# A cross-attention block on one core of Trainium2: all steps of the kernel in another written order

## The chip, the core and the metric

The kernel runs on one core of a Trainium2 chip. A core has five engines that run side by side and wait for each other by semaphores: TensorE (PE, matrix products into PSUM), VectorE (DVE), ScalarE (ACT), GpSimd (POOL) and SyncE (SP, which here only issues DMA transfers). Each engine works through its own list of instructions strictly in the order in which the program emitted them. The time is the device time of one execution, in microseconds (us); several executions give a median and a spread. A profile is the record of one execution.

## The reference

One layer of cross-attention with a feed-forward part, all in fp32: batch B = 4, length L = 512 of both sequences, width D = 512, 16 heads of 32, inner width 2048.

```python
x = layer_norm(hidden_states, ln1_w, ln1_b)
q = (x @ q_w + q_b).reshape(B, LQ, H, HD).transpose(0, 2, 1, 3)
k = (encoder_hidden_states @ k_w + k_b).reshape(B, LK, H, HD).transpose(0, 2, 1, 3)
v = (encoder_hidden_states @ v_w + v_b).reshape(B, LK, H, HD).transpose(0, 2, 1, 3)
scores = jnp.einsum('bhqd,bhkd->bhqk', q, k) * scale
scores = jnp.where(mask, scores, mask_value)
attn = jax.nn.softmax(scores, axis=-1)
out = jnp.einsum('bhqk,bhkd->bhqd', attn, v)
out = out.transpose(0, 2, 1, 3).reshape(B, LQ, D)
out = out @ cproj_w + cproj_b
hidden = out + residual
y = layer_norm(hidden, ln2_w, ln2_b)
y = jax.nn.gelu(y @ fc_w + fc_b, approximate=True)
y = y @ proj_w + proj_b
return residual + y
```

## The kernel before

**Tiles and stages.** The heads of one batch are done in four groups of four, so there are 16 units (batch × group), numbered 0 to 15; each unit has four blocks of 128 query rows. For each unit the kernel projects keys, values and queries, then for each of the four blocks:

- PE computes the scores of four heads into the four PSUM banks `sc` (L581),
- DVE adds the mask and finds the row minimum in one instruction for each head (L589; the scores are negated, so that minimum is the softmax's maximum), which also frees the bank,
- ACT takes the exponential (L592) and sums it,
- DVE turns the result in squares of 32 × 32, two heads at a time (L600, L607; for every second block also L610, the reciprocal of the sums),
- the turned squares change partitions through 12 DMA transfers on SP (`swap<-swap`, issued by the helper at L329) while POOL copies those that stay (L617),
- and after two blocks PE multiplies with the values (L639), and DVE scales the result (L645).

After the four units of a batch come the output projection (L445) with the residual, the second layer norm, the fully connected layer with gelu (L694, L746), whose result goes to DRAM and is read back (`gd`, L748), and at the end of the program the second projection.

**Products in seven instead of eight.** Most large products (keys and values from the second pair of units on, L524, and the fully connected layer, L694) use one level of the Strassen–Winograd scheme: sums of quarters of the weights (POOL) and of the inputs (POOL or DVE), seven smaller products, which are grouped into a chain in one bank and two more in another bank, and a join, in which ACT copies the growing chain out of PSUM three or four times (L720 or, with a bias, L722) and DVE adds the rest (L332). Each product of the chain after the first waits until ACT has copied what stood there. The last projection uses two levels.

**Layer norms.** The statistics of a row block are two DVE instructions (L343, L344). POOL computes the scale from them (L351, L359; named `ve` and `rs`), DVE normalizes the block (L364), and PE turns it (L371) into PSUM, from which DVE or ACT brings it back with weight and bias (L379, L381). For batches 1 to 3 the first layer norm takes another path: the input is also loaded turned (`x_t`), and its statistics are turned on PE (L394) and sent through DRAM (`sd`, L402) so that SP can load them as rows, with which POOL scales the turned input (L412 and L335).

**What sets the order.** All parts are Python generators that emit one piece of their instructions at each step. One string, `ORDER`, names the pieces: each word is a generator (name and indices), and each time a word stands there, that generator makes its next step.

```python
begun = {}
for token in ORDER.split():
    if token not in begun:
        name, *rest = token.split(":")
        begun[token] = takes[name](*map(int, rest))
    if begun[token] is not None:
        next(begun[token], None)
```

So the string sets at once the order on each of the five engines and on the queues of DMA transfers that SP and POOL issue. Words used below: `u:6:0` scores of unit 6, block 0; `x` minima and exponentials; `r` the 32 × 32 turns; `e` exchanges; `d` POOL's copies; `a` attention product; `k:4`, `v:3` key and value products of a pair of units, `kj`, `vj` their joins; `s1`/`s2`, `r1`/`r2`, `n2`, `t2` statistics, scale, normalizing and turning in the two layer norms; `ts` the turned statistics; `es` the sums over the encoder rows; `f`, `j`, `g` fully connected product, join and gelu.

**Buffers.** PSUM has eight banks: four for scores and a ring of four for everything else, which are taken and freed in the written order. The fully connected results go through a few stage buffers (`st`), which are free again once their transfer to `gd` has landed.

Of the kernel before, what the change touches and what calls it, by code (L numbers as in the profile page):

```python
# [20 lines left out]
P = 128  # L21
# [46 lines left out]
u:1:0 kj:1 vj:1 kj:1 k:1 r:0:3 r:0:3 vj:1 v:1 vj:1 lx:1 wq:3 q:3 s1:1 r:0:3 x:1:0 x:1:0 q:3 x:1:0 x:1:0
u:1:1 e:0:0 e:0:0 le:1 e:0:0 lx:1 s1:1 s1:1 r:1:0 wk:4 lh:0 x:1:1 x:1:1 x:1:1 kj:1 x:1:1 kj:1 r:1:1 r:1:0 d:0:1 q:2
  d:0:1 le:1 es:1 vb:0 le:1 lf:0:3 wk:5 le:1 r1:1 es:1 es:1 es:1  # L70
u:1:2 ts:1 ts:1 e:0:1 e:0:1 x:1:2 r:1:1 r:1:1 x:1:2 r:1:1 e:0:1 ks:2 ts:1 ks:2 ks:2 k:2 a:0:0 q:2 x:1:2 x:1:2 a:0:0
  d:1:0
u:1:3 kj:2 x:1:3 x:1:3 k:2 k:2 kj:2 vj:1 r:1:2 x:1:3 x:1:3 r:1:3 r:1:2
u:2:0 x:2:0 r:1:3 wv:4 lt:1 lt:1 lt:1 e:1:0 lb:1 lb:1 a:0:1 k:2 kj:2 v:2 x:2:0 a:0:1 d:1:0 ks:2 na:1 x:2:0 x:2:0
u:2:1 r:1:3 x:2:1 kj:2 e:1:0 e:1:0 na:1 k:2 a:1:0 wa:1 x:2:1 r:1:3 r:2:0 kj:2 x:2:1 x:2:1 wa:1 na:1 r:2:0
u:2:2 x:2:2 wa:1 wq:4 lt:1 na:1 r:2:1 r:2:1 a:1:0 wa:1 x:2:2 x:2:2 d:1:1 q:4 x:2:2 r:2:1 r:2:1 kj:2
u:2:3 x:2:3 vj:2 x:2:3 wq:5 e:1:1 e:1:1 e:1:1 wk:7 wk:6 wv:5 d:1:1 d:2:0 r:2:2 x:2:3 x:2:3 vs:2 ks:3 vs:2 vs:2 ks:3
  vb:1 e:2:0 e:2:0 q:5 e:2:0 wq:7 d:2:0 vs:2 r:2:3 q:4 r:2:3 r:2:2 a:1:1
u:3:0 x:3:0 v:2 v:2 vj:2 a:1:1 x:3:0 r:2:3 x:3:0 x:3:0
u:3:1 x:3:1 x:3:1 r:2:3 r:3:0 a:2:0 v:2 vj:2 x:3:1 x:3:1 a:2:0  # L80
u:3:2 k:3 r:3:0 r:3:1 x:3:2 x:3:2 vj:2 v:2 q:5 r:3:1 x:3:2 kj:3 x:3:2
u:3:3 r:3:1 vj:2 r:3:1 vj:2 x:3:3 d:2:1 vb:1 ks:3 d:2:1 lf:0:0 wq:6 e:2:1 lh:0 e:2:1 e:2:1 e:3:0 e:3:0 e:3:0 wv:6
  x:3:3 d:3:0 d:3:0 s1:2 r:3:2 x:3:3 x:3:3 r:3:2 q:6 a:2:1
u:4:0 m:1 r:3:3 a:2:1 r:3:3 r:3:3 q:7 k:3 x:4:0 x:4:0 q:6 r:3:3 x:4:0 x:4:0
u:4:1 lx:2 r:4:0 wv:7 lt:2 vs:3 ks:3 a:3:0 k:3 x:4:1 q:7 x:4:1 x:4:1 x:4:1
u:4:2 r:4:0 r:4:1 a:3:0 x:4:2 c:0:1 kj:3 k:3 x:4:2 x:4:2 r:4:1 x:4:2 kj:3
u:4:3 lt:2 d:3:1 d:3:1 cb:0 cb:0 r:4:1 vs:3 vs:3 vs:3 r:4:1 d:4:0 vb:2 s1:2 x:4:3 d:4:0 c:0:1 c:0:0 e:3:1 e:3:1 e:3:1
  r:4:2 x:4:3 kj:3 v:3 k:3 lx:2 lf:0:1 lf:0:0 lf:0:3 lh:0 lh:0 cb:0 cb:0 e:4:0 e:4:0 lx:2 e:4:0 lf:0:2 fs:0:0 c:0:0
  r:4:3 kj:3 s2:0 x:4:3 x:4:3 s1:2 a:3:1 vj:3 v:3 v:3 a:3:1 kj:3 r:4:2 r:4:3 vj:3
u:5:0 v:3 r:4:3 s2:0 s1:2 c:0:2 x:5:0 x:5:0 vj:3 r:4:3 vb:2 fs:0:0 r1:2 x:5:0 wv:8 x:5:0 vj:3 r:5:0  # L90
u:5:1 v:3 x:5:1 vj:3 x:5:1 r:5:0 c:0:2 x:5:1 x:5:1 r:5:1 c:0:3 c:0:3 d:4:1 d:4:1 wk:8 le:2 le:2 wk:9 e:4:1 le:2 le:2
  c:0:0 c:0:1 es:2
u:5:2 a:4:0 ts:2 ts:2 k:4 kj:4 r:5:1 x:5:2 s2:0 x:5:2 x:5:2 s2:0 x:5:2 r:5:1 r:5:1 a:4:0 ks:4 es:2 ks:4 es:2 ks:4 ks:4
  es:2 c:0:3 k:4 r2:0 c:0:2 e:4:1 k:4
u:5:3 kj:4 k:4 kj:4 e:4:1 r:5:2 e:5:0 e:5:0 e:5:0 r:5:2 x:5:3 x:5:3 kj:4 vj:3 x:5:3 a:4:1 x:5:3
u:6:0 n2:0 x:6:0 n2:0 k:4 kj:4 n2:0 n2:0 t2:0:3 t2:0:0 t2:0:3 t2:0:0 t2:0:1 t2:0:2 r:5:3 x:6:0 x:6:0 x:6:0 r:5:3
u:6:1 t2:0:1 a:4:1 r:5:3 t2:0:2 kj:4 y:0 y:0 d:5:0 fs:0:0 fs:0:0 fs:0:1 d:5:0 ts:2 fs:0:1 fs:0:1 fs:0:1 a:5:0 y:0
  f:0:1 f:0:0 r:5:3 y:0 j:0:0 j:0:1 x:6:1 a:5:0 x:6:1 r:6:0 f:0:0 f:0:0 f:0:1 x:6:1 x:6:1 f:0:1 j:0:0
u:6:2 f:0:0 j:0:1 j:0:0 lh:1 lt:2 lt:2 wv:9 lb:2 wq:8 lb:2 e:5:1 e:5:1 d:5:1 d:5:1 na:2 r:6:1 r:6:1 r:6:0 f:0:1 j:0:1
  x:6:2 na:2 e:5:1 lx:3 lf:0:2 wk:10 wq:9 j:0:0 f:0:0 na:2 na:2 j:0:0 x:6:2 j:0:1 r:6:1 wa:2 f:0:2 f:0:1 wa:2 j:0:1  # L100
  x:6:2 r:6:2 x:6:2 g:0:0 wa:2 a:5:1
u:6:3 r:6:1 j:0:0 g:0:0 wa:2 q:9 r:6:2 x:6:3 a:5:1 x:6:3 j:0:1 x:6:3 x:6:3
# [918 lines left out]
```

## Time and profile before

| what | us |
|---|---|
| median of 3 runs | 764.81 |
| the runs | 764.81, 766.98, 762.33 |
| the profiled execution | 765.29 |
| its span (first to last instruction) | 763.5 |
| PE busy | 750.3 |
| DVE busy | 614.5 |
| POOL busy | 431.5 |
| ACT busy | 411.4 |

A span is what the profile covers; the time of an execution is 1.8 us longer here. Rows of a profile name the line, the engine, the operation and the tiles, written `out<-in` and without buffer numbers. Where a row ends in brackets, it gives the idle time of that engine just before, and what ended it. The helpers that add, subtract and load have one line each (L332, L335, L329), so such rows are told apart by their tiles: `pbt` holds keys and queries, `ptt` weights and scores, `xn` row blocks, `swap` the turned exponentials, `ext` the turned inputs, `mix` among others the values and the mask. PE's rows count both passes of an fp32 product.

### The profile page before, as it was taken

How to read it: one execution, taken by the hardware profiler on the slowest of the kernel's cores; microseconds unless marked ns; L12 is line 12 of the kernel's file. 1: busy time of each engine (PE TensorE's matmuls, PEld its weight loads, DVE VectorE, ACT ScalarE, POOL GpSimd, SP SyncE). 2: the span in 40 equal slices, each digit the busy share in tenths (PEclk: the TensorE clock that was granted, in tenths of full speed). 3: DMA queues.
4: the chain of work that ended last, by engine and by line, in shares of the span. 5: the costliest groups of instructions: out<-in, count | busy, mean ns of one | idle time of the engine just before them, and what ended most of it. 6: DMA issues, size and time to landing. Idle time of an engine off the chain costs nothing.

```text
span 763.5 us, 14364 instructions
## 1 busy us (share of the span) xinstructions
PE 750.3 (98%) x4953; PEld 548.2 (72%) x4953; DVE 614.5 (80%) x1238; ACT 411.4 (54%) x981; POOL 431.5 (57%) x473
## 2 busy tenths in 40 slices
PE   9999999989999999999999999999999999999998
PEld 6565444646576656776565776767889999999997
DVE  3799999999889889987969787736688789888773
ACT  2567666455998776868867788732234321111111
POOL 1678866876978496889576566894201122131331
PEclk9999999999999999999999999999999999999999
DMA  6788979886777978695785778799535666688565
GB/s 227 236 242 225 236 201 252 232 230 184 242 200 194 281 204 247 196 281 154 214 245 171 218 256 261 215 254 353 167 131 165 214 209 123 213 184 257 140 123 121
DMA packets 72134, 162.19 MB, mean 212 GB/s; under 512 B 11960, under 2 KB 24656, under 8 KB 70400
## 3 DMA queue, kind: packets, MB, share of 16 engines
q1 hardware_dynamic: 56864, 131.44, 58.5%
q0 software_dynamic: 15056, 29.84, 16.0%
q8 instruction: 39, 0.64, 0.3%
q14 instruction: 31, 0.25, 0.1%
q10 hardware_dynamic: 144, 0.02, 0.0%
HBM read 73.95 MB, written 25.18 MB: 130 GB/s over the span
## 4 chain that ended last, share of the span: by engine, by line
PE 87%; DMA 4%; DVE 3%; ACT 3%; SPq 1%; issue 1%; POOL 0%; DVEq 0%; POOLq 0%; ACTq 0%
PE acc L694 36%; PE sc L694 12%; PE acc L524 9%; PE sc L581 8%; PE acc L445 7%; PE acc L639 6%; PE acc L573 5%; DMA ext<-encT_dram 2%; SPq L329 1%; ACT ptt L592 1%; PE acc L371 1%; DVE ptt L589 1%; PE acc L481 1%; PE acc L492 1%; DMA gd<-st 1%
## 5 line engine op out<-in xcount | busy, mean ns | idle before, releaser
L592 ACT ACTIVATE ptt<-ptt,mn 128x512 f32<-128x512 f32 x256 | 182.9, 716 | 52.8 <-DVE mn L589 52.2
L589 DVE CUSTOM_DVE_ANT_0 ptt<-sc,mix 128x512 f32<-128x512 f32 x256 | 165.4, 678 | 21.3 <-PE sc L581 18.6
L617 POOL COPY swap<-swap 32x1088 f32<-32x1088 f32 x128 | 140.2, 1095 | 36.1 <-DVE swap L610 29.6
L720 ACT COPY st<-acc 128x256 f32<-128x256 f32 x128 | 46.1, 367 | 96.3 <-PE acc L694 85.7
L720 ACT COPY xn<-acc 128x128 f32<-128x128 f32 x100 | 24.1, 267 | 133.0 <-PE acc L694 129.3
L600 DVE STREAM_TRANSPOSE swap<-ptt 128x1024 f32<-128x1024 f32 x64 | 79.0, 1235 | 5.2 <-ACT st L746 1.2
L581 PE MATMUL sc<-pbt 32*128 32x512 f32 x512 | 82.0, 647 | 0.0
L607 DVE STREAM_TRANSPOSE swap<-ptt 128x1024 f32<-128x1024 f32 x64 | 78.3, 1223 | 0.6 <-ACT ptt L592 0.6
L748 POOL DMA_DIRECT2D gd<-st x32 | 23.7, 743 | 86.5 <-ACT st L746 65.7
L694 PE MATMUL acc<-ys,ws 128*128 128x256 f32 x256 | 63.4, 383 | 0.5 <-ACT st L720 0.5
L639 PE MATMUL acc<-swap,mix 128*32 128x256 f32 x1024 | 61.9, 382 | 0.9 <-DMA ext<-x_t_dram 0.6
L573 PE MATMUL acc<-ext,ptt 128*128 128x512 f32 x128 | 58.8, 600 | 1.4 <-DVE mn L589 0.8
L445 PE MATMUL acc<-mix 128*128 128x512 f32 x128 | 58.3, 601 | 0.0
L694 PE MATMUL acc<-yT,pbt 128*128 128x256 f32 x240 | 58.1, 383 | 0.0
L694 PEld LDWEIGHTS acc<-ys,ws 128*128 128x128 f32 x256 | 47.4, 190 | 13.1 <-ACT st L720 4.7
L639 PEld LDWEIGHTS acc<-swap,mix 128*32 128x32 f32 x1024 | 30.4, 109 | 33.5 <-issue 9.7
L694 PEld LDWEIGHTS acc<-yT,pbt 128*128 128x128 f32 x240 | 44.5, 190 | 13.7 <-issue 5.1
L906 POOL DMA_DIRECT2D swap<-xn x18 | 22.4, 1434 | 52.8 <-DVE xn L332 18.7
L592 ACT ACTIVATION_READ_ACCUMULATOR ptt<-ptt,mn 128x1 f32 x256 | 48.3, 189 | 0.0
L906 POOL DMA_DIRECT2D yT<-xn x15 | 18.3, 1547 | 48.5 <-DVE yT L332 17.9
L573 PEld LDWEIGHTS acc<-ext,ptt 128*128 128x128 f32 x128 | 23.3, 190 | 30.9 <-issue 23.3
L445 PEld LDWEIGHTS acc<-mix 128*128 128x128 f32 x128 | 23.2, 190 | 31.0 <-issue 28.6
(163 smaller groups left out, 1601.9 us busy)
## 6 DMA issues: line engine op xcount, KB each, us to landing
swap<-swap SPq DMA_DIRECT2D x384, 136.0 KB, 3.3
gd<-st POOLq DMA_DIRECT2D x32, 512.0 KB, 3.9
swap<-gd SPq DMA_DIRECT2D x12, 1024.0 KB, 6.9
pbt<-fc_w_dram SPq DMA_DIRECT2D x40, 256.0 KB, 4.6
xn<-x_dram SPq DMA_DIRECT2D x32, 256.0 KB, 3.9
ext<-fc_w_dram SPq DMA_DIRECT2D x24, 256.0 KB, 3.7
swap<-xn POOLq DMA_DIRECT2D x18, 256.0 KB, 4.7
ptt<-k_w_dram SPq DMA_DIRECT2D x16, 256.0 KB, 5.2
```

Of the source, the lines that this page charges most:

```text
L445: nc.tensor.matmul(acc, oT[:, g, ts(t, P)], wc[:, g, :], start=(g == 0), stop=(g == NG - 1))
L524: nc.tensor.matmul(out_, i, j, start=(k + t == 0 and not more), stop=(k == 1), skip_group_check=more or t > 0)
L573: nc.tensor.matmul(acc, S["wq", w][:, d, :], xT[:, d, :], start=(d == 0), stop=(d == ND - 1))
L581: nc.tensor.matmul(sc[h], S["qT", w][r, ts(qt, P)], S["kT", w][r, :], start=True, stop=True)
L589: nc.vector.tensor_tensor_reduce(out=s, in0=sc[h], in1=mb, scale=1.0, scalar=FMAX, op0=ALU.add, op1=ALU.min, accum_out=mn)
L592: nc.scalar.activation(s, s, AF.Exp, bias=mn, scale=-1.0, accum_out=S["sums", w][:, qt, h : h + 1])
L600: nc.vector.transpose(*two_heads[0])
L607: nc.vector.transpose(*two_heads[1])
L617: nc.gpsimd.tensor_copy(pT[ts(i, HD), i], tb[ts(i, HD), i])
L639: nc.tensor.matmul(av[ts(h, HD), : 2 * P].rearrange(shape, **kw), v[:, t, ts(h, HD)], p[t][h], start=(t == 0), stop=(t == NT - 1),)
L694: nc.tensor.matmul(o, x[:, k], w, start=(k == 0 and not more), stop=(k == n - 1), skip_group_check=more)
L720: nc.scalar.copy(g[:, i], S["qa", *key])
```

## The change

The change replaces the string `ORDER`. The words in it are the same, each as often as before; nearly every line of the string has them in another sequence. The new string is three lines longer, so that every line number further down is higher by three (L589 becomes L592, L364 becomes L367, L332 becomes L335, and L592, the exponential, becomes L595). Two lines of it, as they were and as they are:

```diff
 ORDER = """
...
-u:0:0 x:0:0 x:0:0 x:0:0 x:0:0 wk:3 wv:1 lx:2 wq:1 lx:1 pv:1 wv:2 wq:2 lf:0:1 lx:1 wv:3 lc r:0:0 r:0:0
...
-u:6:0 n2:0 x:6:0 n2:0 k:4 kj:4 n2:0 n2:0 t2:0:3 t2:0:0 t2:0:3 t2:0:0 t2:0:1 t2:0:2 r:5:3 x:6:0 x:6:0 x:6:0 r:5:3
...
+u:0:0 pv:1 lc wv:3 lx:1 wq:2 lf:0:1 lx:1 s1:1 x:0:0 x:0:0 x:0:0 s1:1 x:0:0 r:0:0 r:0:0 ks:1 ks:1 ks:1 vb:0 ks:1 es:0
+  es:0 es:0 es:0 m:0 vs:1 vs:1 pv:1 vs:1 vs:1 vb:0 k:1
...
+u:6:0 a:4:1 r:5:3 t2:0:1 kj:4 r:5:2 x:6:0 a:4:1 x:6:0 f:0:1 t2:0:2 f:0:0 j:0:1 x:6:0 x:6:0 j:0:0 t2:0:2 r:5:3
...
```

Three places are shown as the engines get them.

**DVE, the start of the softmax work.** These are the rows around the first minima (`sc` are score banks, `mn` the minimum, `xn` with `st` and `mv` a row block with its statistics). Before:

```order
L379 TENSOR_SCALAR ext<-acc_78,vec 128x512
L459 TENSOR_SCALAR mix<-m_73 128x512
L567 TENSOR_SCALAR qb<-vec 128x4
L379 TENSOR_SCALAR ext<-acc_78,vec 128x512
L589 ISA ptt,mn_0_0_223<-sc_74,mix 128x512
L589 ISA mn_0_0_223 128x1
L589 ISA ptt,mn_0_1_226<-sc_75,mix 128x512
L589 ISA mn_0_1_226 128x1
L589 ISA ptt,mn_0_2_229<-sc_76,mix 128x512
L589 ISA mn_0_2_229 128x1
```

Now:

```order
L382 TENSOR_SCALAR ext<-acc_81,vec 128x512
L462 TENSOR_SCALAR mix<-m_73 128x512
L570 TENSOR_SCALAR qb<-vec 128x4
L346 BN_STATS st_1_0_254<-xn_86 128x6
L347 BN_AGGR mv_1_253<-st_1_0_254 128x2
L592 ISA ptt,mn_0_0_258<-sc_74,mix 128x512
L592 ISA mn_0_0_258 128x1
L592 ISA ptt,mn_0_1_261<-sc_75,mix 128x512
L592 ISA mn_0_1_261 128x1
L592 ISA ptt,mn_0_2_264<-sc_76,mix 128x512
L592 ISA mn_0_2_264 128x1
L346 BN_STATS st_1_1_267<-xn_87 128x6
```

The statistics of two row blocks of the second batch have moved here, one ahead of the first minimum and one between the third and the fourth (the row that begins it stands last); before, the first of them came behind the twelfth minimum.

**SP, the loads of the second half of the first batch.** The exchanges of the turned exponentials (`swap<-swap`) stand among weight loads, the turned input (`x_t`) and the statistics rows (`sd`). Before:

```order
L329 DMA swap<-swap 32x1088 x12
L329 DMA ptt<-v_w_dram 128x512
L329 DMA ext<-x_t_dram 128x512 x3
L329 DMA swap<-swap 32x1088 x4
L329 DMA xn_87<-sd_99 128x512
L329 DMA xn_82<-sd_99 128x512
L329 DMA swap<-swap 32x1088 x8
L329 DMA ptt<-q_w_dram 128x512
L329 DMA ext<-x_t_dram 128x512
```

Now:

```order
L332 DMA swap<-swap 32x1088 x12
L332 DMA ext<-x_t_dram 128x512
L332 DMA pbt<-fc_w_dram 128x512
L332 DMA ext<-x_t_dram 128x512
L332 DMA xn_86<-sd_99 128x512
L332 DMA xn_87<-sd_99 128x512
L332 DMA swap<-swap 32x1088 x12
L332 DMA ext<-x_t_dram 128x512 x2
L332 DMA ptt<-q_w_dram 128x512 x2
L332 DMA swap<-swap 32x1088 x12
```

The two loads of `sd` stood between four and eight exchanges of one set and now stand ahead of all twelve of it, with loads of `x_t` on both sides. On POOL, the store of `sd` (L402) was issued behind the last three of the four sums over the encoder rows and a weight sum; it now stands behind the first of those four.

**DVE and PE at the second layer norm of the first batch.** On DVE these are minima, the joins of the fifth key pair (L332 with `pbt`) and the normalizations (L364 with `rs`, the scale). Before:

```order
L589 ISA ptt,mn_3_0_1441<-sc_74,mix 128x512
L589 ISA mn_3_0_1441 128x1
L589 ISA ptt,mn_3_1_1444<-sc_75,mix 128x512
L589 ISA mn_3_1_1444 128x1
L332 TENSOR_TENSOR pbt<-acc_78,pbt 128x2x256
L332 TENSOR_TENSOR mix<-acc_79,mix 128x256
L589 ISA ptt,mn_3_2_1449<-sc_76,mix 128x512
L589 ISA mn_3_2_1449 128x1
L589 ISA ptt,mn_3_3_1468<-sc_77,mix 128x512
L589 ISA mn_3_3_1468 128x1
L364 TENSOR_SCALAR xn_85<-xn_85,mv_0_1200,rs_0_1406 128x512
```

Now:

```order
L592 ISA ptt,mn_3_0_1430<-sc_74,mix 128x512
L592 ISA mn_3_0_1430 128x1
L592 ISA ptt,mn_3_1_1433<-sc_75,mix 128x512
L592 ISA mn_3_1_1433 128x1
L367 TENSOR_SCALAR xn_82<-xn_82,mv_0_1257,rs_0_1424 128x512
L367 TENSOR_SCALAR xn_84<-xn_84,mv_0_1257,rs_0_1424 128x512
L367 TENSOR_SCALAR xn_87<-xn_87,mv_0_1257,rs_0_1424 128x512
L335 TENSOR_TENSOR pbt<-acc_78,pbt 128x2x256
L367 TENSOR_SCALAR xn_85<-xn_85,mv_0_1257,rs_0_1424 128x512
L592 ISA ptt,mn_3_2_1481<-sc_76,mix 128x512
L592 ISA mn_3_2_1481 128x1
```

The first three normalizations moved from behind the join to ahead of it, directly behind two minima. On PE, at the same place, are the products of the fifth key pair (L524 with 256 columns), scores (L581) and the turns of the normalized rows (L371). Before:

```order
L524 MATMUL acc_80<-mix,ws_110 128x256 x2
L639 MATMUL acc_81<-swap,mix 32x256 x16
L581 MATMUL sc_74<-pbt 128x512
L581 MATMUL sc_75<-pbt 128x512
L581 MATMUL sc_76<-pbt 128x512
L581 MATMUL sc_77<-pbt 128x512
L524 MATMUL acc_80<-ext,ws_110 128x256 x2
L524 MATMUL acc_78<-mix,ptt 128x256 x2
L371 MATMUL acc_79<-ident,xn_85 128x128
L371 MATMUL acc_79<-ident,xn_83 128x128
L371 MATMUL acc_79<-ident,xn_82 128x128
```

Now:

```order
L397 MATMUL acc_79<-ident,sx_1352 8x128
L527 MATMUL acc_78<-ext,ptt 128x256 x4
L527 MATMUL acc_80<-mix,ws_110 128x256 x4
L527 MATMUL acc_80<-ext,ws_110 128x256 x2
L527 MATMUL acc_78<-mix,ptt 128x256 x2
L374 MATMUL acc_81<-ident,xn_82 128x128
L374 MATMUL acc_81<-ident,xn_84 128x128
L374 MATMUL acc_81<-ident,xn_87 128x128
L374 MATMUL acc_81<-ident,xn_85 128x128
L374 MATMUL acc_79<-ident,xn_82 128x128
L374 MATMUL acc_79<-ident,xn_84 128x128
```

The third, fourth and fifth products of that pair stood with scores, and an attention product, between them and now follow each other; the four turns, 16 products in a row before, have become three turns, then scores, an attention product and a first product of the fully connected layer, and then the fourth.

The ACT engine has two loads of its function table fewer in the new order (726 instead of 728 instructions), because exponentials and gelu alternate less often. All other instructions are the same in number on every engine.

More of the change, by code (lines that the diff above doesn't have):

```diff
@@ L68 @@
[L68 to L95, printed above, removed]
-u:6:0 n2:0 x:6:0 n2:0 k:4 kj:4 n2:0 n2:0 t2:0:3 t2:0:0 t2:0:3 t2:0:0 t2:0:1 t2:0:2 r:5:3 x:6:0 x:6:0 x:6:0 r:5:3
@@ L97 @@
[L97 to L102, printed above, removed]
```

290 lines of the change are left out of this document (163 added, 127 removed).

## The prediction

> **What bounds the kernel now.** I read the summary first, then busy time in stretches, then the waits of each engine, and single rows last. The summary seems to leave nothing to gain, since TensorE (PE) is busy for nearly the whole span:
>
> ```profile
> span 763.5 us, 14364 instructions
> PE 750.3 (98%) x4953; PEld 548.2 (72%) x4953; DVE 614.5 (80%) x1238; ACT 411.4 (54%) x981; POOL 431.5 (57%) x473
> ```
>
> The stretches correct that (start:end, length, then busy time of PE, weight loads, VectorE (DVE), ScalarE (ACT), GpSimd (POOL), the granted clock):
>
> ```profile
> 40.00:60.00 20.00, 20.00 (x122) 11.91 (x124) 19.29 (x42) 12.06 (x34) 15.04 (x15) 1.00 0.85 241
> 160.00:180.00 20.00, 17.06 (x125) 9.56 (x125) 18.91 (x36) 11.03 (x28) 14.83 (x19) 0.91 0.57 166
> 180.00:200.00 20.00, 19.22 (x113) 13.61 (x114) 19.20 (x41) 14.40 (x33) 17.73 (x17) 1.00 0.86 239
> 200.00:220.00 20.00, 20.00 (x116) 13.41 (x115) 14.72 (x33) 18.86 (x44) 16.83 (x18) 1.00 0.78 234
> ```
>
> In the stretches between 40 and 200 us DVE is busy for about 19 of 20 us; from 200 us on PE is busy throughout, with DVE well below. So the span has two bounds, DVE first and PE behind it. That PE is not at its own pace in the first part shows in how long one set of scores (four heads) takes. Columns from here on: start, length, engine, line, operation, and in brackets the idle time ahead and what ended it.
>
> ```profile
> 56.42 1.14 PE L581 MATMUL sc<-pbt 32*128 32x512 f32 x8
> 60.42 3.18 PE L581 MATMUL sc<-pbt 32*128 32x512 f32 x8
> ```
>
> The second set is the same work, held by DVE, which has not yet read the banks that it overwrites. The profile books such a wait as busy time. The open waits of PE are few; two of them (us in total, times, longest):
>
> ```profile
> PE acc L573 <- DVE mn L589: 0.8, 1, 0.8
> ...
> PE acc L694 <- ACT st L720: 0.5, 1, 0.5
> ```
>
> What decides the time is therefore when DVE has done the work that PE needs up to about 200 us, where the 0.8 for a score minimum (L573) is PE's last wait of that part. Up to there a microsecond of DVE idle time, or of DVE work moved out of the chain, is worth a microsecond at the end; PE's waits are not to be added to it. DVE's own waits from its first minimum on:
>
> ```profile
> DVE ptt L589 <- PE sc L581: 5.4, 5, 4.5
> DVE pbt L332 <- ACT pbt L722: 1.0, 2, 0.8
> DVE swap L600 <- DMA ext<-x_t_dram: 0.8, 1, 0.8
> DVE ptt L589 <- DVE swap L600: 0.5, 3, 0.2
> DVE ptt L589 <- ACT ptt L592: 0.3, 2, 0.2
> DVE swap L600 <- ACT ptt L592: 0.3, 1, 0.3
> DVE st L332 <- ACT st L720: 0.2, 1, 0.2
> DVE swap L600 <- DMA swap<-swap: 0.2, 1, 0.2
> DVE swap L600 <- DMA ptt<-k_w_dram: 0.2, 1, 0.2
> ```
>
> The 4.5 stands ahead of the first minimum. Without it and without the 0.5 that DVE pays behind its own transposes, 3.9 us can be lost there at all, 0.9 of them waits for scores.
>
> **The change part by part.** Every engine has the same work as before, only in another order. The sum is made against the profiled execution, 765.29 us with a span of 763.5; the median of the runs is 764.81, which is 0.48 lower.
>
> *Start of the DVE chain.* The row statistics (L343, L344) of the second batch's first row block stand ahead of the first minimum now. They took:
>
> ```profile
> 158.09 0.69 DVE L343 BATCH_NORM_STATS2 st<-xn 128x6 f32<-128x512 f32 x1
> ...
> 158.91 0.66 DVE L589 CUSTOM_DVE_ANT_0 ptt<-sc,mix 128x512 f32<-128x512 f32 x1
> ```
>
> From 158.09 to the next start at 158.91 that is 0.82 us, and it fits into the 4.5 us idle. What follows is 0.82 us less in the chain: −0.82. The load of that row block is moved ahead of a weight load that waits on PE, so it is not later. The second pair goes between the third and the fourth minimum; it only changes its place within the chain, which costs nothing. The bounds are −0.82 and 0.
>
> *The queue of loads (SP).* Before, three loads, four exchanges, the two statistics rows (sd, which POOL stores and SP loads) and eight exchanges stood in that order:
>
> ```profile
> 60.81 0.61 POOL L402 DMA_DIRECT2D sd<-xn  x1
> ...
> 62.79 2.42 SPq L329 DMA_DIRECT2D swap<-swap  x4
> 65.31 1.81 SPq L329 DMA_DIRECT2D xn<-sd  x2
> ```
>
> Further on, on DVE:
>
> ```profile
> 76.69 1.25 DVE L600 STREAM_TRANSPOSE swap<-ptt 128x1024 f32<-128x1024 f32 x1 [0.78 <-DMA ext<-x_t_dram]
> ```
>
> The exchange came in two pieces with 1.81 us of sd issue between them, and the DVE transpose at 76.69, which writes the buffer that the exchange reads, waited 0.78 us. Now the two sd loads stand ahead of all twelve exchanges, which follow each other, so the second piece needs no 1.81 us behind the first. For that the sd loads must be able to go earlier. They went 4.5 us after POOL's store (65.31 − 60.81). POOL now stores ahead of three sums over the encoder (1.27 us each by the row at 157.34 below), 3.8 us, so at about 57.0, and the loads can go at 61.5, ahead of the first exchange at 62.79. The 1.3 us between are the cover. I take the whole wait as gone: −0.78. If the cover fails and the loads stay at 65.31, all twelve exchanges come behind them, four of them at 2.42 us more than before: the bounds are −0.78 and +2.4.
>
> *A join that waited.* The join of the fifth key pair (L332, k:4) waited for an ACT copy:
>
> ```profile
> 164.31 1.13 PE L524 MATMUL acc<-mix,ws 128*128 128x256 f32 x4 [0.67 <-ACT pbt L722]
> ...
> 165.99 0.69 DVE L332 TENSOR_TENSOR pbt<-acc,pbt 128x512 f32<-128x512 f32 x1 [0.76 <-ACT pbt L722]
> ...
> 168.15 0.91 DVE L364 TENSOR_SCALAR xn<-xn,mv,rs 128x512 f32<-128x512 f32 x1
> ```
>
> Three normalizations (L364) stand ahead of that join now, 0.91 us each by the row at 168.15, so the copy has over two more microseconds: −0.76. For this the normalizations need their scale earlier, and that comes from POOL behind the sums over the encoder rows:
>
> ```profile
> 157.34 1.27 POOL L335 TENSOR_TENSOR mix<-ext,mix 128x512 f32<-128x512 f32 x1 [3.67 <-DMA ext<-encT_dram]
> ...
> 164.11 1.04 POOL L359 TENSOR_TENSOR rs<-ve,nhalf 128x4 f32<-128x4 f32 x1
> ```
>
> The scale was done at 165.15 and used at 168.15, 3.0 us of cover. Without the join pair ahead of it and one of the two pairs of minima, DVE gets there 2.9 us earlier (168.15 less the 165.23 at which the earlier minima end, 165.99 − 0.76). The cover shrinks to about 0.1. I take it as just enough, since POOL issues no store between those sums and the scale any more; the bounds are −0.76 and, if POOL's wait of 3.67 for the encoder comes a second time and only the 0.1 covers it, +3.6.
>
> *PE around there.* The third to fifth products of k:4 stand back to back, without scores between them, so PE waits for two more copies, at 0.67 each by the row at 164.31. DVE is the bound there and PE has slack until about 200 us: 0, bounds 0 and +1.3. Of the four turns of normalized rows (L371) three now stand ahead of the scores and one behind an attention product and a fully connected one. Here the clock matters:
>
> ```profile
> 171.20:174.50 3.30, 1.61 (x11) 0.95 (x10) 3.30 (x4) 1.00 (x2) 3.20 (x5) 1.00 0.11 26
> 174.50:177.90 3.40, 3.40 (x16) 1.73 (x15) 3.40 (x10) 2.87 (x8) 0.97 (x2) 0.50 0.33 99
> ```
>
> The columns are those of the stretches above. After 3.30 us in which PE worked for 1.61 (turns alone) its clock was 0.50 for 3.40 us, so 1.70 us of PE's work was lost. DVE was busy for all 3.40 of it, so I count 0 for keeping or losing this. [...]
>
> *Table loads.* Exponentials and gelu stand in somewhat longer runs, so two loads of ACT's function table fall away:
>
> ```profile
> L746 ACT ACT_TABLE_LOAD x21 | 26.9, 1283 | 0.4
> ```
>
> That is 2 × 1.283 = 2.57 us of ACT, an engine that is busy for 54% of the span and not the bound: 0, bounds −0.6 (DVE's waits for exponentials) and 0.
>
> *After 200 us.* PE is the bound. The pieces are shuffled over hundreds of rows, but with the same weights, sums and stores ahead of each. PE's one wait there (0.5 for a stage copy) may go or be joined by others: 0, bounds −0.5 and the rival below. POOL, busy for 57% of the span, gets stores and sums in another order; I count 0 for it, within the same bounds.
>
> The sum is −0.82 − 0.78 − 0.76 = −2.4 us: 762.9 for an execution like the profiled one, and 764.81 − 2.4 = 762.4 at the median.
>
> **The rivals.**
>
> *All of DVE's waits go.* A new order could also remove the other waits in the list. Its rows leave 0.8 + 1.0 + 0.3 + 0.3 + 0.2 + 0.2 + 0.2 = 3.0; with the 0.9 of score waits, the 0.82 at the start and PE's 0.5 (L694) this gives −5.2, so 759.6. For it speaks that each of these is one wait of 0.2 to 0.8 us; against it, that a new order makes new ones.
>
> [...]
>
> *The scale comes late.* The bound of the join step: the cover of 0.1 us is used up, DVE waits up to 3.6 us ahead of L364, and the sum is −2.4 + 3.6 = +1.2, 766.0, on the other side of before. It decides as soon as POOL's scale ends later than DVE's minima ahead of it.
>
> *Stage buffers.* From 200 us on, fully connected results go through a few stage buffers, and the copy out of PSUM waits until the store of an earlier one has landed:
>
> ```profile
> ACT st L720 <- DMA gd<-st: 10.5, 7, 4.0
> ```
>
> Before, only 0.5 of these 10.5 us reached PE. The copies free PSUM banks, so if the new order has no other product at hand there, the rest would come through: up to −2.4 + 10.0, 772.4; half of it gives 767.4. It decides where a copy has less than about 4 us of other PE work behind it. Against it: seven waits cost PE only 0.5.
>
> **How the numbers follow.** The forecast (762.4, give or take 1.5) has 0.36, all waits gone 0.34, the kept clock 0.06, the late scale 0.08, stage buffers or another such wait on PE 0.16. A change of 0.5%, 3.8 us, is about what a measurement here can tell from none, so faster means below 761.0 and slower above 768.6. The second and third case are faster (0.40), the first and fourth the same (0.44), the last slower (0.16). The range runs from 758.1, the 759.6 with the same 1.5, to 767.0, which holds the late scale with 1.0 to spare and leaves out most of the last case.
>
> **What would show it.** In the profile of the changed kernel: two pairs of statistics ahead of and between the first four minima, and the idle time ahead of the first minimum shorter by 0.8; no wait of a transpose near 76 us; three L364 rows (three lines further down) directly behind two minima, without idle time, and the join behind them without its 0.76; DVE's last bound stretch ending 2 to 3 us earlier, and PE solid from there. Wrong would be: idle time on DVE ahead of those normalizations; waits of PE on stage copies after 200 us; PE's waits between 60 and 200 us the same in sum although DVE's went.

## The result: 0.96% slower, mostly by a wait near 440 us that the forecast's sum left at 0

The changed kernel took 772.11 us at the median of 7 executions (770.11 to 776.6), the kernel before 765.42 us beside it on the same chip. The ratio is 1.0096, with a 95% interval of 1.0067 to 1.0125: slower by 6.7 us between medians, where the forecast was 762.4 with a range up to 767.0. Line numbers of the changed kernel are three higher than those of the kernel before (L723 is what L720 was).

The profiled execution of the changed kernel is its slowest one, 776.6 us. Its span and its busy engines, from the page:

```profile
span 774.7 us, 14396 instructions
...
PE 755.8 (98%) x4953; PEld 550.9 (71%) x4953; DVE 618.5 (80%) x1238; ACT 408.9 (53%) x979; POOL 433.7 (56%) x473
```

TensorE is busy for 98% of a span that is 11 us longer, with the same 4953 matmul instructions (two passes for each fp32 product). The sum of busy time again tells nothing, because products at a halved clock and products that wait for a bank count as busy (four products took 2.05 us at 443.38 where such four take 1.03; in the kernel before eight scores that waited for banks took 3.18 us at 60.42 where such eight take 1.14). The stretches of 20 us show where it is (from:to, length, busy time and instructions of PE, weight loads, DVE, ACT and POOL, then PE's granted clock, the DMA share and GB/s):

```profile
60.00:80.00 20.00, 17.06 (x129) 9.78 (x128) 18.16 (x39) 14.38 (x36) 18.00 (x17) 0.91 0.89 228
80.00:100.00 20.00, 19.12 (x87) 9.18 (x86) 17.56 (x41) 11.97 (x32) 12.89 (x14) 0.85 0.83 222
160.00:180.00 20.00, 16.65 (x105) 9.95 (x105) 19.53 (x38) 10.47 (x29) 15.31 (x18) 1.00 0.66 190
440.00:460.00 20.00, 16.60 (x76) 11.86 (x76) 8.70 (x22) 11.80 (x27) 6.88 (x9) 0.83 0.68 213
```

The last of these stretches in the kernel before:

```profile
440.00:460.00 20.00, 19.46 (x125) 14.58 (x126) 16.19 (x35) 16.48 (x39) 12.46 (x16) 1.00 0.76 253
```

From 440 to 460 us PE, DVE and POOL now all stand for part of the time and PE's clock is low. PE's longest waits (us in total, times, longest):

```profile
PE acc L697 <- POOL ws L338: 3.6, 1, 3.6
PE acc L642 <- DMA swap<-swap: 2.2, 1, 2.2
```

The first is in that stretch, the second at 72.38 us. On PE's timeline the first one looks like this (start, duration, instruction, count, and in brackets the idle time ahead of it and what ended it):

```profile
443.38 2.05 PE L697 MATMUL acc<-ys,ws 128*128 128x256 f32 x4 [3.60 <-POOL ws L338]
445.36 2.09 PE L584 MATMUL sc<-pbt 32*128 32x512 f32 x8
447.38 1.95 PE L697 MATMUL acc<-ys,ws 128*128 128x256 f32 x4
```

Four such products take 1.03 us elsewhere, eight such scores 1.14. Here they take 2.05 and 2.09: after the wait PE ran at half clock (0.50 granted from 443.38 to 446.80 us). The wait cost more than its own 3.6 us.

To see the whole span by the same measure I use "lost time": a stretch of the span less the work that PE began in it, where each product counts with the usual distance of products of its shape in the trace of before (0.43 us for 128 by 512, 0.22 for 128 by 256, and so on). It holds open waits, hidden ones and low clock alike. Stretches in us, one profiled execution each:

| kernel | to 200 | 200–400 | 400–540 | behind | whole |
|---|---|---|---|---|---|
| before | 28.9 | 6.2 | 4.2 | 0.2 | 39.5 |
| after | 28.6 | 7.4 | 14.9 | −0.3 | 50.7 |

The first 200 us, where the forecast's terms lie, lost as much as before in this execution. Of 11.2 us more, 10.7 lie between 400 and 540 us.

### The profile page after: what moved, and what is told of

Same layout as the page of the kernel before. It is cut to its first block, busy times and chain, and to the rows that moved or that the text cites. A ratio compares the mean times of both kernels' runs of the same rounds, so it can differ in the third digit from the quotient of the medians.

```text
span 774.7 us, 14396 instructions
## 1 busy us (share of the span) xinstructions
PE 755.8 (98%) x4953; PEld 550.9 (71%) x4953; DVE 618.5 (80%) x1238; ACT 408.9 (53%) x979; POOL 433.7 (56%) x473
## 4 chain that ended last, share of the span: by engine, by line
PE 72%; POOL 7%; DVE 5%; DMA 4%; issue 4%; SPq 4%; ACT 3%; DVEq 0%; POOLq 0%
PE acc L697 27%; PE sc L697 11%; PE acc L527 10%; PE sc L584 7%; PE acc L448 5%; PE acc L576 5%; PE acc L642 5%; SPq L332 4%; POOL swap L620 2%; ACT ptt L595 2%; POOL ws L338 1%; DVE ptt L592 1%; DMA ptt<-q_w_dram 1%; DVE xn L367 1%; PE acc L495 1%
## 5 line engine op out<-in xcount | busy, mean ns | idle before, releaser
L595 ACT ACTIVATE ptt<-ptt,mn 128x512 f32<-128x512 f32 x256 | 182.8, 715 | 56.2 <-DVE mn L592 54.9
L592 DVE CUSTOM_DVE_ANT_0 ptt<-sc,mix 128x512 f32<-128x512 f32 x256 | 164.9, 677 | 26.7 <-PE sc L584 20.3
L723 ACT COPY st<-acc 128x256 f32<-128x256 f32 x128 | 46.1, 367 | 110.3 <-PE acc L697 72.7
L723 ACT COPY xn<-acc 128x128 f32<-128x128 f32 x100 | 24.3, 268 | 129.9 <-PE acc L697 127.8
L751 POOL DMA_DIRECT2D gd<-st x32 | 24.2, 758 | 113.2 <-ACT st L749 67.1
L909 POOL DMA_DIRECT2D swap<-xn x18 | 23.7, 1448 | 60.3 <-DVE xn L335 22.1
L595 ACT ACTIVATION_READ_ACCUMULATOR ptt<-ptt,mn 128x1 f32 x256 | 48.2, 188 | 0.0
L584 PEld LDWEIGHTS sc<-pbt 32*128 32x128 f32 x512 | 25.1, 185 | 32.1 <-DVE mn L592 12.6
L749 ACT ACTIVATE st<-st,vec 128x512 f32<-128x512 f32 x64 | 44.1, 718 | 3.0 <-DVE st L335 2.4
```

The lines of the kernel that those rows point to most:

```text
L584: nc.tensor.matmul(sc[h], S["qT", w][r, ts(qt, P)], S["kT", w][r, :], start=True, stop=True)
L592: nc.vector.tensor_tensor_reduce(out=s, in0=sc[h], in1=mb, scale=1.0, scalar=FMAX, op0=ALU.add, op1=ALU.min, accum_out=mn)
L595: nc.scalar.activation(s, s, AF.Exp, bias=mn, scale=-1.0, accum_out=S["sums", w][:, qt, h : h + 1])
L723: nc.scalar.copy(g[:, i], S["qa", *key])
```

## The experiments

Each kernel was run beside runs of the kernel before on the same chip. Times are medians; the ratio is to those runs, with its 95% interval; the last three columns are the lost time of the one profiled execution, from 0, 200 and 400 us on.

| run | time | ratio | to 200 | 200–400 | 400–540 |
|---|---|---|---|---|---|
| e1, early order new | 766.14 | 1.0033 [1.0006, 1.0060] | 25.8 | 10.2 | 4.8 |
| e2, late order new | 772.79 | 1.0129 [1.0088, 1.0171] | 26.1 | 11.1 | 8.7 |
| e3, after, one store later | 765.01 | 1.0017 [0.9995, 1.0039] | 25.7 | 7.8 | 7.3 |
| e4, before with the three steps | 768.54 | 1.0054 [1.0025, 1.0082] | 28.6 | 8.2 | 4.8 |
| e5, two of the steps | 763.17 | 0.9986 [0.9960, 1.0012] | 24.5 | 6.7 | 5.0 |
| e6, the third step alone | 768.03 | 1.0042 [1.0014, 1.0070] | 31.8 | 6.8 | 4.6 |
| e7, after, zeros behind the wait | 772.47 | 1.0105 [1.0070, 1.0140] | 24.3 | 7.6 | 11.0 |
| e8, e3 with three more words moved | 770.19 | 1.0059 [1.0038, 1.0080] | 29.9 | 8.6 | 7.3 |
| e9, after, zeros at the wait | 772.39 | 1.0104 [1.0076, 1.0133] | 24.2 | 7.6 | 10.0 |
| e10, after, store of g:1:3 by ACT | 766.36 | 1.0031 [1.0011, 1.0050] | 26.8 | 7.7 | 7.1 |
| e11, e5 early, e3 late | 772.85 | 1.0112 [1.0085, 1.0140] | 24.4 | 13.5 | 6.9 |
| e12, after, store of g:1:4 by ACT | 766.54 | 1.0022 [1.0000, 1.0045] | 23.7 | 7.6 | 7.3 |
| e13, e5, four stores by ACT | 772.01 | 1.0091 [1.0055, 1.0127] | 29.2 | 8.5 | 12.9 |
| e14, after, both stores by ACT | 764.83 | 0.9993 [0.9969, 1.0017] | 26.7 | 8.1 | 5.8 |

The lost time of e7 and e9 leaves out the 3.0 us of work that they add. Executions of one order differ: after's order up to 200 us stands in eight of these profiles (after, e1, e3, e7, e9, e10, e12, e14), with 23.7 to 28.6, mean 25.7. They were taken on different chips.

### Early or late: e1 and e2

Theory A, as the expectations call it: the loss comes from the late part of the order, from the word `u:13:0` on (about 390 us). Its rival puts it into the early part. e1 takes after's order up to that word and before's behind it, e2 the other way round; words that one order has earlier than the other stand at the seam.

> The changed order up to the scores of unit 13, block 0 (about 388 us), then the rest in the order of before. Theory A (the loss lies behind 400 us, where POOL brings weight sums late and PE waits 3.6 us and then runs at half clock; the first 200 us give nothing and cost nothing): 764 to 767 us, and no wait of PE above 1.5 us behind 390 us. Rival B (the first 200 us lose, by new waits of DVE that sum to 9 us against 4 before): 769 to 773 us.

> The reverse: the order of before up to the scores of unit 13, block 0, then the rest in the changed order. Theory A: 769 to 773 us, with the 15 us wait of POOL for a gelu near 400 to 416 us, and the wait of PE for a weight sum of 2 to 4 us near 440 us. Rival B: 764 to 766 us.

e1 took 766.14, e2 772.79, as theory A has it: most of the loss comes with the late part. The two sides are not pure, though. Both have a loss at the seam that neither whole order has: 10.2 and 11.1 us between 200 and 400, where before and after have 6.2 and 7.4. So about half of what e2 loses more than before is made by the seam (4.9 us between 200 and 400, with a wait of PE of 3.10 us at 386.12), and 4.5 us lie between 400 and 540. There the wait is found again: PE stands for 2.56 us until 443.29, this time at full clock (1.00 from 440 to 460 us).

### The store that POOL waits for: e3

In the trace of after, POOL (its timeline) stands for 15.14 us ahead of a store, and then has work without a gap for 27 us, in which stand the sums for `fs:1:4` to `fs:1:7` and, 20 us on, the store of the next gelu:

```profile
416.15 0.73 POOL L751 DMA_DIRECT2D gd<-st  x1 [15.14 <-ACT mix L608]
...
436.44 0.97 POOL L751 DMA_DIRECT2D gd<-st  x1
...
442.66 0.72 POOL L338 TENSOR_TENSOR ws<-ws,pbt 128x256 f32<-128x256 f32 x1
```

The store at 416.15 is the third step of `g:1:3`, which must wait for its gelu on ACT; that ends at 415.66, and the profile names a copy right behind it. In the order before the store stands behind sums for `fs:1:4`, and POOL does not wait for it:

```profile
416.90 0.74 POOL L335 TENSOR_TENSOR ws<-pbt,ws 128x256 f32<-128x256 f32 x1
417.57 0.74 POOL L748 DMA_DIRECT2D gd<-st  x1
```

In the new order it stands ahead of them. e3 moves this one word:

```diff
-x:13:3 x:13:3 g:1:3 fs:1:4 fs:1:4 c:2:0 ... vb:7 fs:1:5 fs:1:5 vb:7
+x:13:3 x:13:3 fs:1:4 fs:1:4 c:2:0 ... vb:7 fs:1:5 fs:1:5 g:1:3 vb:7
```

> The changed order with one word moved: the last step of g:1:3, POOL's store of a gelu result, goes behind the sums of fs:1:4 and fs:1:5. Theory A: POOL does sums where it waited 15 us, the wait of PE near 440 us falls from 3.6 to below 1 us, its clock stays full there, and the time is 3.6 (the wait) to 6.6 us (wait and half clock) below the changed kernel, 765.5 to 768.5 us. Rival C (POOL's sums there wait for the loads of their weights, not for the store): the idle time only gets another name, and the time stays at 771 to 773 us.

It took 765.01: one word of 2,569 takes back 7.1 us between medians, 6.0 by the two ratios. POOL begins its sums after 9.82 us idle instead of 15.14, and PE's wait falls to 0.44:

```profile
408.30 0.74 POOL L335 TENSOR_TENSOR ws<-pbt 128x256 f32<-128x256 f32 x1 [9.82 <-DMA pbt<-p_w_dram]
...
413.83 0.73 POOL L751 DMA_DIRECT2D gd<-st  x1
```

```profile
437.19 1.10 PE L697 MATMUL acc<-ys,ws 128*128 128x256 f32 x4 [0.44 <-POOL swap L620]
```

That shows which word costs the time. It does not show through which wait, because this move brings forward both POOL's sums and the stores behind them.

### Filling PE's wait: e7 and e9

Both add seven products of 128 by 128 by 256 with a tile of zeros, 3.0 us of work, to a chain of the fully connected layer; they add 0 to the sum. e7 has them ahead of the third product of `f:1:7`, e9 of `f:1:6`:

```diff
+        if (b, c) == (1, 6):
+            for _ in range(7):
+                nc.tensor.matmul(chain, zero, y11[:, 0], start=False, stop=False, skip_group_check=True)
         product(chain, s2, t2, True)
```

> The kernel after with seven more products of 128 by 128 by 256 with a stationary tile of zeros (they add 0 to the sum), set ahead of the third product of f:1:7, so that TensorE works while it would have stood for 3.6 us for the weight sum of POOL. Wait and clock both count (theory A): the wait for POOL stays, as work instead of idleness, the clock stays at 1.0 behind it, and the time is 3 us below after, 768 to 770. If the low clock behind the wait costs nothing (all 7 us come from late weight sums), the time is that of after, 771 to 773; if the fillers end later than the awaited sum, it is above after by what they go beyond it.

> As the run with the seven zero products, but ahead of the third product of f:1:6, which is the one that waits (the run before had them ahead of f:1:7's, behind the wait). The seven take some 3.0 us and fill a wait of 3.4 to 3.6 us. If the halved clock behind the wait is 3 us of the loss (theory A), the wait stays as work, the clock stays at 1.00 in 440 to 460 us, and the time is 2 to 3 us below after, 769 to 770; if the clock costs nothing, or is gone only because the profiled run of after was its slowest, 771 to 773.

Neither helped, and e7 was misplaced: the product that waits is that of `f:1:6`, ahead of the zeros. e9 was placed right and did not do what it was meant to: the zeros themselves waited. PE's and ACT's timelines of e9 (four lines further down than after, so L727 is ACT's copy out of the chain):

```profile
439.07 3.29 PE L714 MATMUL acc<-yT,zero 128*128 128x256 f32 x14 [3.48 <-ACT st L727]
442.20 1.03 PE L698 MATMUL acc<-ys,ws 128*128 128x256 f32 x4
```

```profile
438.64 0.37 ACT L727 COPY st<-acc 128x256 f32<-128x256 f32 x1 [5.54 <-DMA gd<-st]
```

A product with zeros reads no weight sum. What it needs is that ACT has copied the chain's bank, and ACT's copy stood for 5.54 us, until a store of an earlier stage buffer had landed. e7's wait is put down to the same copy:

```profile
438.99 2.04 PE L698 MATMUL acc<-ys,ws 128*128 128x256 f32 x4 [3.38 <-ACT st L727]
```

So the page of after named the wrong releaser. There the copy is just as late:

```profile
431.87 2.59 ACT L749 ACTIVATE st<-st,vec 128x512 f32<-128x512 f32 x4
...
442.86 0.37 ACT L723 COPY st<-acc 128x256 f32<-128x256 f32 x1 [5.56 <-DMA gd<-st]
```

It ends at 443.23, 0.15 us ahead of the product at 443.38. POOL's sum at 442.66 ends at 443.38 to the hundredth, and was named because it came last. By the program it belongs to `fs:1:7`, which the waiting product of `f:1:6` doesn't read; the sums of `fs:1:6` were done by 433.1.

The chain is then: the store of `g:1:3` holds POOL, so the store of `g:1:4`, whose gelu is done by 434.46 (431.87 + 2.59), is issued only at 436.44; its stage buffer is free when it has landed, 6.3 us later, and `j:1:6` takes that buffer. The trace gives the 5.56 us of ACT as a wait for just this transfer.

### Which of the two waits: e12, e10 and e14

These leave after's order as it is and let ACT, which has just computed the gelu, issue a store in place of POOL: e12 that of `g:1:4`, e10 that of `g:1:3`, e14 both.

```diff
-        nc.gpsimd.dma_start(out=gd[b][:, :, c], in_=g.rearrange(...))
+        (nc.scalar if (b, c) == (1, 4) else nc.gpsimd).dma_start(out=gd[b][:, :, c], in_=g.rearrange(...))
```

> The kernel after, in its own order, with one store moved to ScalarE's queue: that of g:1:4, which frees the stage buffer st_88. The store of g:1:3 stays ahead of POOL's sums, so POOL keeps its 15 us hold and its sums come as late as before. Theory S (the third product of f:1:6 waits for j:1:6's first copy, which waits for the stage buffer that g:1:4's store frees, and that store stands 20 us deep in POOL's line): the wait of 3.5 us near 440 and what follows it go, 765 to 768. Theory W (the product waits for POOL's late weight sum, as the page of after names it): nothing changes, 771 to 773.

> The kernel after, in its own order, but the store of g:1:3 is issued by ScalarE, which has just made the gelu, in place of POOL: no word is moved and POOL has no wait there. If POOL's 15 us behind that store are what makes the late part slower (theory A), the time is that of the run with the moved store, 764 to 767, and POOL begins the sums of fs:1:4 some 5 us earlier; if the moved store had helped by another change that came with it (the order of the loads or of the sums), 770 to 773.

> The kernel after with the stores of both g:1:3 and g:1:4 issued by ScalarE. If the stage buffer is the whole of the 6 to 7 us (theory S), this is no better than either store alone, 765 to 767. If POOL's hold has a price of its own beside it, below the better of the two by more than 1 us, 763 to 765.

e12 took 766.54, 5.6 below after, as theory S has it. POOL still stands for 15.14 us, and the sum that after's page had named still ends late, at 437.20, where PE has long gone on:

```profile
410.86 0.73 POOL L751 DMA_DIRECT2D gd<-st  x1 [15.14 <-ACT mix L608]
...
436.48 0.72 POOL L338 TENSOR_TENSOR ws<-ws,pbt 128x256 f32<-128x256 f32 x1
```

```profile
431.73 2.75 PE L697 MATMUL acc<-yT,pbt 128*128 128x256 f32 x12
434.32 1.03 PE L697 MATMUL acc<-ys,ws 128*128 128x256 f32 x4
435.28 1.14 PE L584 MATMUL sc<-pbt 32*128 32x512 f32 x8
```

The same products as in after, without the wait and at full clock (1.00 from 420 to 460 us). ACT's copy waits 1.00 us for the buffer instead of 5.56:

```profile
433.00 0.37 ACT L723 COPY st<-acc 128x256 f32<-128x256 f32 x1 [1.00 <-DMA gd<-st]
```

Counted from the start of the gelus, e12 issues the store 2.6 us earlier than after (428.56 − 426.58 against 436.44 − 431.87), and it lands 4.4 us after its issue instead of 6.3. Together that is the 4.56 us by which the copy's wait shrank; why it landed faster is not shown.

So the stage buffer is the cause, shown by undoing it alone, and POOL's late sum is not. e10 (766.36) stands level with it. e14 (764.83) is 1.5 us below e10, which by the expectation would give POOL's hold a price of that size beside the buffer; the intervals of the two ratios overlap, so this stays open.

What the wait is worth can be read twice. Between medians it is 5.6 to 7.3 us (after less e12, e10, e3, e14; 5.0 to 7.9 by their ratios). In the profile it is 3.60 of wait and (2.05 − 1.03) + (2.09 − 1.14) + (1.95 − 1.13) = 2.8 of half clock on the three groups of products behind it, 6.4 us. That the two agree is partly chance, since the half clock is not in every execution. The mean granted clock of the whole span is 0.988 in the profiled execution and 0.998 in two others of after (772.76 and 772.11 us), which leaves less than 2 us there for all drops together (0.0025 × 772). How the loss divides into wait and clock stays open.

### The three forecast steps: e4, e5, e6

e4 makes the three moves on which the forecast's sum rests in the order before, and no others. e5 makes the first two, e6 the third:

```diff
-u:0:0 x:0:0 x:0:0 x:0:0 x:0:0 ... lx:2 wq:1 lx:1 ...          (e4, e5: first row block and its statistics)
+lx:1 u:0:0 s1:1 x:0:0 x:0:0 x:0:0 x:0:0 ... lx:2 wq:1 ...
-... es:1 es:1 es:1 ... ks:2 ts:1 ks:2 ks:2 ... e:1:0 lb:1 lb:1  (e4, e5: sd stored and loaded earlier)
+... es:1 ... ts:1 es:1 es:1 ks:2 ks:2 ks:2 ... lb:1 lb:1 e:1:0
-x:5:3 x:5:3 kj:4 ... u:6:0 n2:0 x:6:0 n2:0 k:4 kj:4 n2:0 n2:0   (e4, e6: normalizations ahead of the join)
+x:5:3 x:5:3 n2:0 n2:0 n2:0 kj:4 ... u:6:0 x:6:0 k:4 kj:4 n2:0
```

> The order of before with only the three steps on which the forecast summed: the first statistics pair ahead of the first minimum, the sd store and loads earlier, three normalizations ahead of the join of k:4. By the forecast DVE's waits of 0.78 (near 77 us) and 0.76 us (near 166 us) are gone, the chain is 0.82 us shorter, and the time is 2.4 us below before, 763.0 us. Rival D (each gain is taken back by the next thing that is late on PE or DVE before 200 us): within 1 us of before, with new waits of DVE that sum to about what went.

> The kernel before with two of the three forecast steps: the statistics pair ahead of the first minimum, and the sd loads ahead of the twelve exchanges; the three normalizations stay behind kj:4. The forecast's terms would give -0.82 - 0.78 = -1.6 us against the kernel before. Rival, from the run with all three steps (the gain of the start was kept to 149 us, and the 0.78 us wait came back as 0.29 + 0.27 + 0.53): the start's 0.82 kept and the rest given back, -0.8 to 0. If the run with three steps was slower (+4.8 between medians) because of these two, this one is slower too, by 2 us and more.

> The kernel before with one forecast step alone: the three n2:0 ahead of the kj:4 of the same pair. The forecast's term: -0.76 us, and no other change. New theory: VectorE now does the three normalizations ahead of the minima of u:6:0, so TensorE's scores wait for a minimum (near 168 us, 2 us) and the turns of t2:0 come later, with a VectorE wait of 3 to 4 us for them near 177 us; the time is +1 to +3 us.

With all three the kernel was slower (768.54), with the first two 1.5 us below before (763.17; the interval of the ratio, 0.9960 to 1.0012, takes in no change), with the third alone 3.4 us above it (768.03). So the third term has the wrong sign, and the first two agree with the size that the forecast gave, but the time alone doesn't show them. Part of the 1.5 can be the clock: eight of e5's ten executions had a mean granted clock of 0.999 or 1.000, and 14 of the 29 of before beside it; between these alone the medians differ by 1.1 us. In e5, DVE starts its first minimum 0.91 us earlier, at 23.39 after 3.73 us idle, where before it was 24.30 after 4.55:

```profile
23.39 0.69 DVE L589 CUSTOM_DVE_ANT_0 ptt<-sc,mix 128x512 f32<-128x512 f32 x1 [3.73 <-PE sc L581]
```

With the wait of 0.78 gone, DVE is some 1.8 us ahead of before near 76 us (a minimum at 76.30 instead of 78.11). A transpose then waits 0.53 us at 86.55 for a load, and 1.20 us of the lead are left at 149 us. The same minimum in before and in e5:

```profile
148.97 0.69 DVE L589 CUSTOM_DVE_ANT_0 ptt<-sc,mix 128x512 f32<-128x512 f32 x1 [0.28 <-PE sc L581]
```

```profile
147.77 0.69 DVE L589 CUSTOM_DVE_ANT_0 ptt<-sc,mix 128x512 f32<-128x512 f32 x1 [0.27 <-PE sc L581]
```

What the third step does is in e6's rows of POOL, DVE and PE:

```profile
165.07 0.73 POOL L451 DMA_DIRECT2D xa<-xn  x1
```

```profile
169.07 1.04 DVE L364 TENSOR_SCALAR xn<-xn,mv,rs 128x512 f32<-128x512 f32 x1 [2.93 <-DMA xa<-xn]
```

```profile
171.70 2.56 PE L581 MATMUL sc<-pbt 32*128 32x512 f32 x4 [3.37 <-DVE mn L589]
```

The third normalization works in place on a row block whose store POOL issued at 165.07, and waits 2.93 us for it to land. Behind it on DVE stand the last two minima of `u:5:3`. PE's second half of the scores of `u:6:0` overwrites their banks, waits 3.37 us for them and then takes 2.56 us instead of 1.13 for the four, as at half clock (0.83 is the mean granted from 160 to 180 us, where before has 0.91). That is no single case: all ten executions of e6 have a mean granted clock of 0.998 or less, 0.994 on average, where before has 0.999 on average beside it. Over 765 us that difference is an estimated 3.5 us of PE's work, about what e6 is slower. In e4 the stores landed in time and no normalization waited, yet three of them took 2.55 us ahead of the same minima, and the scores still waited 2.15.

### Versions meant to be better: e8, e11, e13

e8 is e3 with `fs:1:7` ahead of the store of `g:1:4`, `wq:4` earlier and the products of `a:1:0` behind `k:2`. e11 is e5 up to `u:13:0` and e3 from there. e13 is e5 with the stores of `g:1:3` to `g:1:6` issued by ACT.

> The kernel after with the moved g:1:3 store, and three more words moved out of the way of a wait that after's trace shows: two fs:1:7 ahead of the store of g:1:4 (TensorE's wait of 0.44 us near 437), wq:4 behind the first lt:1 (its 0.75 to 1.82 us wait for a load of q_w near 79), and the products of a:1:0 behind k:2 (their 2.19 and 1.28 us wait for an exchange near 72). If these waits are what the new early order costs, 1 to 3 us below the run with the store alone, 762 to 764 where before is 764 to 765; if they are made good elsewhere or move to other products, the time stays at 765.

> A version from the parts that did well: the kernel before with the start and the sd loads moved, up to u:13:0, and from there after's order with the store of g:1:3 behind the sums. The start and the sd loads gave -1.5 between medians. If after's late order is worth what the run with the moved store hints at (1.1 us less than the run of after's early with before's late order), the sum is -2.6 against before, 761 to 763; if the late order is worth nothing, it is -1.5, 762.5 to 764; if the seam makes a new wait, as it did for after's late order behind before's early one (3.1 us near 390), 765 and more.

> A version meant to beat both: the kernel before with the start and the sd loads moved (763.2 in its run, before 764.7), and the stores of g:1:3 to g:1:6 issued by ScalarE. In that run's trace ScalarE waits 1.2 us for stage buffers and POOL stands 14 us for gelus at these stores, none of it with more than 0.6 us on TensorE. If TensorE's waits for staged copies (0.52 us near 443) are all that there is to gain, 762.5 to 763; if the earlier stores let the later weight sums and loads come forward too, 761 to 762; if ScalarE's issues (0.6 us each) delay its exponentials, 764.

None beats the kernel before. In e8 the products of `k:2` now wait, 4.05 us where the moved ones had waited 2.19; in e11, whose line numbers are three lower than those of before, the seam waits:

```profile
75.13 1.91 PE L527 MATMUL acc<-ext,ws 128*128 128x256 f32 x4 [4.05 <-ACT ptt L595]
```

```profile
387.07 2.08 PE L521 MATMUL acc<-ws,mix 128*128 128x128 f32 x8 [5.89 <-ACT mix L717]
```

e13 made the same mistake as the change itself on another queue. The store of `g:1:5`, whose gelu ended at 440.38, was issued by ACT at 444.89, because it stood behind exponentials and copies in the written order. It then took 8.6 us to land, where the other three that ACT issued took 3.2 to 4.9; why is not shown. PE waited for the buffer:

```profile
453.55 0.37 ACT L720 COPY st<-acc 128x256 f32<-128x256 f32 x1 [7.34 <-DMA gd<-st]
```

```profile
454.07 2.04 PE L694 MATMUL acc<-ys,ws 128*128 128x256 f32 x4 [5.82 <-ACT st L720]
```

The best of all is e5, not to be told apart from the kernel before.

## Why the prediction was wrong, step by step

- **Start of the DVE chain (−0.82).** Held. In after the first minimum starts at 23.11, 1.19 us earlier than the 24.30 of before, and in e5 the gain is there as well.
- **The queue of loads (−0.78).** The wait of 0.78 at 76.69 is gone in e5. In after a transpose waits 0.33 for an exchange at 72.36, and another 1.30 at 87.07, where the profile names a load of weights (`ptt<-v_w_dram`). Of this step and the one ahead of it, −1.6 together, DVE's rows in e5 keep 1.20 to 149 us; the −1.5 between e5's medians agrees, with an interval that takes in none and the clock as a rival.
- **A join that waited (−0.76, bounds to +3.6).** Failed as a step by itself: e6 is 3.4 us slower, near the upper bound but by another way. The forecast asked whether the scale would be there in time, and counted 0 for what stands behind the moved normalizations on DVE, the minima for which PE waits. In after the step does little harm, since much else there moves with it:

```profile
166.32 3.60 DVE L367 TENSOR_SCALAR xn<-xn,mv,rs 128x512 f32<-128x512 f32 x3 [0.29 <-POOL rs L362]
```

  The scale was 0.29 us late, so the cover of 0.1 was judged nearly right.
- **PE around there (0).** The clock of 160 to 180 us was 1.00 in after, with the turns three and one, where before had 0.91. The kept clock, the third case with its 0.06, was the author's estimate, and no run shows that the order of the turns keeps the clock: e1 and e3, with after's order there, had 1.00 and 0.91, and e5, with the turns as in before, 1.00. That PE would not be the worse for new waits elsewhere failed: the attention product at 72.38 is put ahead of its exchange and waits 2.19 us, with a clock of 0.91 and 0.85 in the two stretches around it. Over the eight executions with this order the first 200 us lost 25.7 us at the mean, with 28.9 and 26.1 in the two that have the order of before; a gain of 1 to 2 us is likely there, not shown.
- **After 200 us (0, bounds −0.5).** This is the step that failed: it counted 0 where the runs show 5 to 8 us. It rested on "the same weights, sums and stores ahead of each", and on 0 for POOL, because POOL is busy for 57%. The stores do not have the same ahead of them: one stands behind a store that waits 15.14 us for another engine. The bound of −0.5 was made from the waits that were there, and said nothing of those that could come.
- **The rival on stage buffers (772.4, chance 0.16).** This is what happened, by mechanism and time: the copy out of PSUM waits for a store to land, and PE has no other product at hand. Its time was met by luck: it set up to 10.0 us of waits, spread over seven copies, against gains of 2.4. What came was one wait of 5.56 us on ACT, 3.60 of them on PE, with 2.8 of half clock behind it in the profiled execution, beside gains that mostly did not come. What spoke against it, "seven waits cost PE only 0.5", was no evidence for an order in which the stores themselves are issued at other times.

Not explained: mended (e3, e10, e12, e14) the new order still loses 5.8 to 7.3 us between 400 and 540 us, against 4.2 to 5.0 with before's order there, and 1 to 2 us more than before between 200 and 400 (where e4, with before's order there, lost 8.2 too). In the waits this shows as several of 0.7 to 1.2 us (a POOL sum near 475, a load of the fully connected weights or an exchange near 502 to 515). Which words bring them was not tried.

## What to carry to other kernels

When a change reorders everything, do not price a stretch at zero because its mean load is low: go through each in-order queue for an instruction that waits for another engine, and list what stands behind it, transfers above all, since a late store keeps a buffer, and a buffer keeps the engine that is the bound (here the copy on ACT for 5.56 us, and by it PE for 3.60). When a wait has several semaphores, test the one that the profile names by freeing the others alone; here the wrong one ended 0.15 us behind the right one. A step that removes a wait on one engine must be followed to the next consumer in that engine's list before its saving counts.

## What the runs showed of the hardware

Behind a wait of PE of nearly the same length the clock was halved in one run and full in another. In after and in e9 PE waited at the same place; these are the wait and the 3.4 us behind it, in the columns of the stretches above (the clock is the third number from the end):

```profile
439.78:443.38 3.60, 0.00 (x1) 0.03 (x1) 0.25 (x1) 0.52 (x2) 3.43 (x4) 0.84 0.94 337
443.38:446.80 3.42, 3.42 (x12) 1.67 (x12) 1.31 (x2) 2.22 (x6) 0.73 (x1) 0.50 1.03 341
```

```profile
435.58:439.07 3.49, 0.01 (x1) 0.00 (x1) 0.26 (x1) 0.42 (x2) 3.32 (x4) 1.00 1.02 368
439.07:442.40 3.33, 3.33 (x15) 2.96 (x16) 1.31 (x2) 1.94 (x5) 0.84 (x2) 1.00 0.96 315
```

Behind 3.60 us the clock was 0.50, behind 3.49 it was 1.00, and behind the 3.38 of e7 four products took 2.04 us instead of 1.03. It was low behind a shorter wait too: behind the 2.19 us at 72.38 in after the clock was 0.68 for 3.4 us:

```profile
72.40:75.80 3.40, 3.40 (x34) 2.03 (x35) 3.40 (x7) 1.39 (x4) 2.31 (x2) 0.68 0.78 238
```

So the length of a wait alone does not tell the clock behind it in these runs; what decides it is not shown.

And executions of one written order differ by several microseconds in the first 200 us (23.7 to 28.6 of lost time), more than each forecast step was worth. A single profile could not have told a step of 0.8 us from none by its total; its rows could.
